# Two wide blocks in place of three narrow ones: re-tiling the expert stage of a fused cross-attention and mixture-of-experts kernel

## The chip, the core and the metric

The kernel runs on one core of a Trainium2 chip. Its engines work side by side, each on its own queue of instructions: TensorE (PE: matrix products and transposes, written to PSUM), VectorE (DVE), ScalarE (ACT), GpSimd (POOL, which here issues gathers and scatters by index) and SyncE (SP, which here issues the plain DMAs). PSUM has 8 banks of 512 fp32 numbers per partition. The metric is the time of one execution on the device in microseconds (us); the kernel before takes 9008.61 us (median of 3 runs, 9005.31 to 9009.49).

## The reference

Everything is fp32. `x` is 4 x 1024 tokens of width 1024. The first layer adds an attention map of each token, computed against a context. The second layer, which takes nearly all the time, is a mixture of 8 experts, of which each token uses 2:

```python
x = x + attention(layernorm(x), ctx_512, ...)
...
router_probs = softmax(x_flat @ gate_w)
topk_w, topk_idx = top_k(router_probs, 2)
topk_w = topk_w / sum(topk_w, axis=-1)
# each token goes to its two experts, sorted by expert
h = silu(ragged_dot(x_rep_sort, w1, group_sizes)) * ragged_dot(x_rep_sort, w3, group_sizes)
out_sort = ragged_dot(h, w2, group_sizes)
out = einsum('tkd,tk->td', out_rep, topk_w)
```

`w1` and `w3` are 1024 x 3584 for each expert, `w2` is 3584 x 1024. The 4096 tokens make 8192 token-expert pairs. On these inputs the router gives the eight experts 984, 991, 1080, 994, 1047, 1004, 1046 and 1046 of them.

## The kernel before

**First part** (up to about 500 us): layer norms, attention, the router, and lists of slots: which token sits where in which expert. At its end small DVE operations on one row (L513 to L564) work out for each expert a *run*: the expert, its first slot and its kind, where a kind is a pair (blocks, width) out of the table `RUNS` (L23). A kind holds blocks x width tokens; the smallest that holds an expert's tokens is taken. Before, the large kinds are three blocks of a width in steps of 8.

**Expert stage** (L566 on). A loop over the runs (L896) switches on the kind (L900) into code unrolled for that kind, `run(i, ex, s0, blocks, width)` (L794). Every matrix product is done by Strassen's scheme in Winograd's form: 7 products of half size, `p1` to `p7`, in place of 8. The tokens of a block are split into two halves of n = width / 2 columns, the other two dimensions into halves as well. So each product has n columns of moving operand, a stationary tile of 128 x 128, and needs sums of weights (`weight_sums`, L627, four DVE operations on a loaded tile) and sums of tokens. fp32 products are two MATMUL instructions each.

A block has two stages:

- *Stage 1* (L813): for each of NI = 14 pairs of 128 hidden units, w1 and then w3: load a weight tile of 1 MB (SP), make its sums, do 7 products of 4 steps of the contraction each (L825), and put the result together from PSUM with `combine` (L657: one ACT copy, four DVE adds). Then silu (ACT), times (DVE), and `token_sums` (L645) stores seven planes of the hidden tile `g`: four quarters, of which one is overwritten by a sum, and three sums.
- *Out-projection* (L853): for each of DQ = 4 quarters of the output width, the 14 pairs in *units* of a weight tile (`W2K`: 8, 8, 6 and 6 times 128 hidden units), 7 products a pair (L864) accumulated over all pairs, `combine`, and for each tile of 128 tokens (`tokens_out`, L767) two transposes on PE (L774), a DVE operation that scales and adds them to `acc` (L776), and, after the last quarter, a scatter to the output by POOL (L780). `acc` was gathered from the output at the end of stage 1 (L851), since another expert may have written there.

The next block's tokens are gathered by POOL into `rows` at the block's begin (L811), or, for the next run's first block, after stage 1 (L844, `load_first`: rows and the first weight tiles `w1a` and `w3a`, which have buffers of their own). `tokens_in` (L737) transposes them on PE into `x` in the out-projection, behind the second quarter. These steps, transposes in and out, stand in a list `late` and are taken from it one by one between products, after each pair of the out-projection or each product group of stage 1. What is left over at the end of a run is done by the next run (`leftover`, L791), after the last run behind the loop.

**What sets the order.** PE's order is as written (`manual_schedule`, L901). On the other engines the framework orders the instructions when it builds the program, and each engine's queue is then executed in order. PSUM: six banks for product groups (a group takes four, two products to a bank except `p1`), two for transposes. Weight tiles go round in three buffers. At the loop's end all engines meet before the next run begins.

Of the kernel before, what the change touches and what calls it, by code (L numbers as in the profile page):

```python
# [19 lines left out]
P = 128  # L20
N = 512

RUNS = [(1, 192), (1, 376), (2, 288), (2, 376), (3, 288)]  # L23
RUNS += [(3, w) for w in range(320, 377, 8)]
# [10 lines left out]
def kernel(  # L35
# [540 lines left out]
    with ExitStack() as st:  # L576
        fst = st.enter_context(tc.tile_pool(name="fst", bufs=1))
        wp = st.enter_context(tc.tile_pool(name="wp", bufs=3))
        hp = st.enter_context(tc.tile_pool(name="hp", bufs=1))
        gp = st.enter_context(tc.tile_pool(name="gp", bufs=2))  # L580
        ip = st.enter_context(tc.tile_pool(name="ip", bufs=2))
        ps = st.enter_context(tc.tile_pool(name="ps", bufs=6, space=PSUM))
        pst = st.enter_context(tc.tile_pool(name="pst", bufs=2, space=PSUM))
# [4 lines left out]
        W2K = [8, 8, 6, 6]  # L588
# [3 lines left out]
        XW = RT * P  # L592
        assert all(w // 2 <= NM and w <= XW for _, w in RUNS)


        T1, B11, B12, B21, B22, T2, T4 = range(7)
        T3 = B12
# [9 lines left out]
        def load(wf, ex, k0, kn, c0):  # L607
            t = wp.tile([P, KD, QW], F32, tag="w", name="wt")
            weights(t, wf, ex, k0, kn, c0)
            return t  # L610

        def factors(t, kn, halves, s):

# [13 lines left out]
        def weight_sums(t, kn, halves, s=None):  # L627
            if s is None:
                s = wp.tile([P, 3, HK, P], F32, tag="s", name="ws")
            f = factors(t, kn, halves, s)  # L630
            a11, a12, a21, a22 = f["p1"], f["p2"], f["p7"], f["p4"]
            nc.vector.tensor_tensor(f["p5"], a21, a22, ALU.add)  # L632
            nc.vector.tensor_tensor(f["p6"], f["p5"], a11, ALU.subtract)  # L633
            nc.vector.tensor_tensor(f["p3"], a12, f["p6"], ALU.subtract)  # L634
            nc.vector.tensor_tensor(a21, a11, a21, ALU.subtract)  # L635
            return f

        RIGHT = dict(p1=B11, p2=B21, p3=B22, p4=T4, p5=T1, p6=T2, p7=T3)
        BANK = dict(p1=(0, 0), p2=(1, 0), p6=(1, 1), p5=(2, 0), p7=(2, 1), p3=(3, 0), p4=(3, 1))
        ENDS = ["p1", "p6", "p7", "p4"]  # L640
# [4 lines left out]
        def token_sums(v, n):  # L645

            def two(a, b):
                return v[..., a : b + 1 : b - a, :]

            nc.vector.tensor_tensor(two(T1, T3), two(B12, B22), two(B11, B12), ALU.subtract)  # L650
            nc.vector.tensor_tensor(v[..., T2, :], v[..., B22, :], v[..., T1, :], ALU.subtract)
            nc.vector.tensor_tensor(v[..., T4, :], v[..., B21, :], v[..., T2, :], ALU.subtract)

        def banks():
            return [ps.tile([P, N], F32, tag="ps", name=f"ps{i}") for i in range(4)]

        def combine(pp, n, c, wide):  # L657

            def pair(t):
                return t[:, : 2 * n].rearrange("p (a b) -> p a b", b=n)  # L660

            def twice(v):
# [3 lines left out]
            nc.scalar.copy(p1s, pp[0][:, :n])  # L666
            nc.vector.tensor_tensor(pair(c), pair(pp[1]), twice(p1s), ALU.add)  # L667
            vu = gp.tile([P, 2, n], F32, tag="vu", name="vu")
            nc.vector.tensor_tensor(vu, pair(pp[2]), twice(c[:, n : 2 * n]), ALU.add)  # L669
            mid = c[:, n : 2 * wide - n].rearrange("p (a b) -> p a b", b=wide - n)[:, :, :n]  # L670
            nc.vector.tensor_tensor(mid, pair(pp[3]), vu, ALU.add)  # L671
            nc.vector.tensor_tensor(  # L672
                c[:, wide + n : wide + 2 * n], pp[2][:, :n], vu[:, 1, :], ALU.add
            )

# [32 lines left out]
        rd0 = fst.tile([P, RT], I32, name="rd0")  # L708
        rows = [fst.tile([P, D], F32, name=f"rows{s}") for s in range(RT)]
        w1a = fst.tile([P, KD, QW], F32, name="w1a")  # L710
        w3a = fst.tile([P, KD, QW], F32, name="w3a")
# [221 lines left out]
```

## Time and profile before

| | us |
|---|---|
| three runs of the kernel | 9008.61 (9005.31 to 9009.49) |
| the profiled execution | 9005.26 |
| its span, first to last instruction | 9003.5 |
| up to the first product of the first run | 535.4 |
| first run (n = 164) / second (168) / third (180) | 999.2 / 1022.7 / 1093.7 |
| between two runs | 10.4 to 11.2 |
| after the last run's products | 16.9 |

The profile is of one execution; all times in it are of that one. Busy time of PE is no measure of its speed, since matmuls overlap: what counts is the distance from one start to the next. Columns of a group are: line, engine, operation, output and inputs with their shapes, count, busy us, mean ns of one, and idle time of the engine before them with what ended it. The mean granted clock of PE over the whole span was 0.987 of full speed.

### The profile page before, as it was taken

How to read it: one execution, taken by the hardware profiler on the slowest of the kernel's cores; microseconds unless marked ns; L12 is line 12 of the kernel's file. 1: busy time of each engine (PE TensorE's matmuls, PEld its weight loads, DVE VectorE, ACT ScalarE, POOL GpSimd, SP SyncE). 2: the span in 40 equal slices, each digit the busy share in tenths (PEclk: the TensorE clock that was granted, in tenths of full speed). 3: DMA queues.
4: the chain of work that ended last, by engine and by line, in shares of the span. 5: the costliest groups of instructions: out<-in, count | busy, mean ns of one | idle time of the engine just before them, and what ended most of it. 6: DMA issues, size and time to landing. Idle time of an engine off the chain costs nothing. (4 is left out here: it accounts for less than half of the span.)

```text
span 9003.5 us, 140017 instructions
## 1 busy us (share of the span) xinstructions
PE 8812.5 (98%) x59462; PEld 8651.3 (96%) x59463; DVE 5109.8 (57%) x10101; ACT 698.5 (8%) x1528; POOL 412.4 (5%) x496
## 2 busy tenths in 40 slices
PE   8979999999999999999999999999999999999999
PEld 5579999999999999999999999999999999999999
DVE  5665655655655655556556556456565565555554
ACT  3310000000000000000000000000000000000000
POOL 2310000000000000000000000000000000000000
PEclk9989999999999999999999999999999999999999
DMA  3234444444443444444444434444444444434343
GB/s 139 109 132 145 139 147 146 138 149 136 154 130 120 144 135 139 133 139 141 142 134 143 142 124 137 145 131 151 142 145 133 129 140 137 140 129 144 125 140 126
DMA packets 1115213, 1236.38 MB, mean 137 GB/s; under 512 B 35312, under 2 KB 1075184, under 8 KB 1114416
## 3 DMA queue, kind: packets, MB, share of 16 engines
q1 hardware_dynamic: 1081616, 1118.37, 38.3%
q0 software_dynamic: 32656, 107.24, 3.4%
q8 instruction: 501, 8.21, 0.4%
q14 instruction: 296, 2.42, 0.1%
q10 hardware_dynamic: 144, 0.13, 0.0%
HBM read 1155.26 MB, written 73.53 MB: 136 GB/s over the span
## 5 line engine op out<-in xcount | busy, mean ns | idle before, releaser
L825 PE MATMUL ps<-x,wt 128*128 128x168 f32 (+3 forms) x15744 | 2510.6, 309 | 0.0
L825 PEld LDWEIGHTS ps<-x,wt 128*128 128x128 f32 x15744 | 2351.7, 190 | 0.0
L864 PE MATMUL ps<-g,wt 128*128 128x168 f32 (+3 forms) x10752 | 2070.9, 309 | 0.0
L632 DVE TENSOR_TENSOR ws<-wt 128x512 f32<-128x512 f32 (+1 forms) x1040 | 693.7, 667 | 2120.1 <-DMA wt<-in_L_ffn_w_dram 2042.2
L864 PEld LDWEIGHTS ps<-g,wt 128*128 128x128 f32 x10752 | 1691.4, 190 | 0.0
L825 PE MATMUL ps<-xs,ws 128*128 128x168 f32 (+3 forms) x10624 | 1659.2, 309 | 0.0
L864 PE MATMUL ps<-g,ws 128*128 128x168 f32 (+3 forms) x8064 | 1615.3, 309 | 0.0
L825 PEld LDWEIGHTS ps<-xs,ws 128*128 128x128 f32 x10624 | 1579.0, 190 | 0.0
L864 PEld LDWEIGHTS ps<-g,ws 128*128 128x128 f32 x8064 | 1294.7, 190 | 0.0
L667 DVE TENSOR_TENSOR c<-ps,p1s 128x352 f32<-128x352 f32 (+3 forms) x672 | 346.5, 516 | 1030.9 <-PE ps L825 1000.1
L825 PE MATMUL ps<-x,ws 128*128 128x168 f32 (+3 forms) x5312 | 883.2, 309 | 0.0
L825 PE MATMUL ps<-xs,wt 128*128 128x168 f32 (+3 forms) x5248 | 872.5, 309 | 0.0
L825 PEld LDWEIGHTS ps<-x,ws 128*128 128x128 f32 x5312 | 804.0, 190 | 0.0
L825 PEld LDWEIGHTS ps<-xs,wt 128*128 128x128 f32 x5248 | 794.3, 190 | 0.0
L633 DVE TENSOR_TENSOR ws<-ws,wt 128x512 f32<-128x512 f32 (+1 forms) x1040 | 692.0, 665 | 28.4
L635 DVE TENSOR_TENSOR wt<-wt 128x512 f32<-128x512 f32 (+1 forms) x1040 | 685.7, 659 | 0.0
L634 DVE TENSOR_TENSOR ws<-wt,ws 128x512 f32<-128x512 f32 (+1 forms) x1040 | 684.6, 658 | 0.0
L666 ACT COPY p1s<-ps 128x168 f32<-128x168 f32 (+3 forms) x768 | 228.2, 297 | 4658.8 <-PE ps L864 2341.3
L836 ACT ACTIVATE c<-c 128x672 f32<-128x672 f32 (+3 forms) x336 | 261.5, 778 | 2648.0 <-DVE c L671 2626.8
L671 DVE TENSOR_TENSOR c<-ps,vu 128x352 f32<-128x352 f32 (+3 forms) x672 | 344.6, 513 | 28.5 <-PE ps L825 20.8
L669 DVE TENSOR_TENSOR vu<-ps,c 128x352 f32<-128x352 f32 (+3 forms) x672 | 342.3, 509 | 5.7 <-PE ps L825 5.6
L699 POOL DMA_INDIRECT rows<-h_d,rd x75 | 79.7, 1063 | 4880.1 <-DVE ws L633 2278.0
(186 smaller groups left out, 3746.1 us busy)
## 6 DMA issues: line engine op xcount, KB each, us to landing
wt<-in_L_ffn_w_dram SPq DMA_DIRECT2D x848, 1024.0 KB, 5.1
wt<-in_L_ffn_w_dram SPq DMA_DIRECT2D x192, 768.0 KB, 4.7
xt<-in_x_dram SPq DMA_DIRECT2D x32, 512.0 KB, 4.3
out_dram<-x SPq DMA_DIRECT2D x32, 512.0 KB, 2.9
h_d<-hn SPq DMA_DIRECT2D x32, 512.0 KB, 2.6
w1a<-in_L_ffn_w_dram SPq DMA_DIRECT2D x9, 1024.0 KB
w3a<-in_L_ffn_w_dram SPq DMA_DIRECT2D x9, 1024.0 KB
cx<-in_ctx_dram SPq DMA_DIRECT2D x4, 1024.0 KB
```

Of the source, the lines that this page charges most:

```text
L632: nc.vector.tensor_tensor(f["p5"], a21, a22, ALU.add)
L633: nc.vector.tensor_tensor(f["p6"], f["p5"], a11, ALU.subtract)
L634: nc.vector.tensor_tensor(f["p3"], a12, f["p6"], ALU.subtract)
L635: nc.vector.tensor_tensor(a21, a11, a21, ALU.subtract)
L666: nc.scalar.copy(p1s, pp[0][:, :n])
L667: nc.vector.tensor_tensor(pair(c), pair(pp[1]), twice(p1s), ALU.add)
L669: nc.vector.tensor_tensor(vu, pair(pp[2]), twice(c[:, n : 2 * n]), ALU.add)
L671: nc.vector.tensor_tensor(mid, pair(pp[3]), vu, ALU.add)
L699: nc.gpsimd.indirect_dma_start(out=dst, out_offset=None, in_=src, in_offset=bass.IndirectOffsetOnAxis(ap=rd[:n, s : s + 1], axis=0),)
L825: nc.tensor.matmul(pp[bk][:, ts(half, n)], left[p][:, k, :], right[p][:, k, :], start=(k == 0), stop=(k == HK - 1),)
L836: nc.scalar.activation(c1, c1, AF.Silu)
L864: nc.tensor.matmul(pp[bk][:, ts(half, n)], left[p][:, k, :], g[:, i2, RIGHT[p], :], start=(i2 == 0 and half == 0), stop=(i2 == NI - 1 and ...
```

## The change

The large kinds are two blocks of a width from 480 to 564 in steps of 4. Each of the seven products has a PSUM bank (seven banks, the eighth for transposes). `rows` takes the part of `acc` too, `w1a` and `w3a` go, and the weights go round in three fixed buffers, into which the first two tiles of the next run are loaded behind the last load of a run. The hidden tile `g` has four planes in place of seven; three sums are made in the out-projection, for each pair and each quarter again (`hidden_factors`), into four small buffers. The units of the out-projection are 4, 6, 6, 6 and 6 times 128; in the last of them the products are done product by product, in the others pair by pair. The next rows are gathered at the fifth pair of stage 1 in both cases, transposed from the start of the out-projection on, and each tile of `rows` is then filled from the output. There are five row tiles, the last of 64 rows, where there were three.

```diff
-RUNS = [(1, 192), (1, 376), (2, 288), (2, 376), (3, 288)]
-RUNS += [(3, w) for w in range(320, 377, 8)]
+RUNS = [(1, 192), (1, 376), (1, 564), (2, 376), (2, 432)]
+RUNS += [(2, w) for w in range(480, 565, 4)]
...
-        wp = st.enter_context(tc.tile_pool(name="wp", bufs=3))
+        tp = st.enter_context(tc.tile_pool(name="tp", bufs=4))
...
-        ps = st.enter_context(tc.tile_pool(name="ps", bufs=6, space=PSUM))
-        pst = st.enter_context(tc.tile_pool(name="pst", bufs=2, space=PSUM))
+        ps1 = st.enter_context(tc.tile_pool(name="ps1", bufs=1, space=PSUM))
+        ps2 = st.enter_context(tc.tile_pool(name="ps2", bufs=3, space=PSUM))
+        pst = st.enter_context(tc.tile_pool(name="pst", bufs=1, space=PSUM))
...
-        W2K = [8, 8, 6, 6]
+        W2K = [4, 6, 6, 6, 6]
+        WR = 3
...
+        ROWS = [P, P, P, P, P // 2]
...
         def banks():
-            return [ps.tile([P, N], F32, tag="ps", name=f"ps{i}") for i in range(4)]
+            one = ps1.tile([P, N], F32, tag="ps1", name="ps1")
+            two = [ps2.tile([P, 2, N], F32, tag="ps2", name=f"ps2_{i}") for i in range(3)]
+            pp = dict(p1=one)
+            for t, (a, b) in zip(two, (("p2", "p6"), ("p5", "p7"), ("p3", "p4"))):
+                pp[a], pp[b] = t[:, 0, :], t[:, 1, :]
...
         rows = [fst.tile([P, D], F32, name=f"rows{s}") for s in range(RT)]
-        w1a = fst.tile([P, KD, QW], F32, name="w1a")
-        w3a = fst.tile([P, KD, QW], F32, name="w3a")
-        s1a = fst.tile([P, 3, HK, P], F32, name="s1a")
+        wts_in = [fst.tile([P, KD, QW], F32, name=f"w{j}") for j in range(WR)]
+        sums_in = [fst.tile([P, 3, HK, P], F32, name=f"s{j}") for j in range(WR)]
...
-        acc = [fst.tile([P, D], F32, name=f"acc{s}") for s in range(RT)]
-        for a in acc:
-            nc.vector.memset(a, 0.0)
...
+        def hidden_factors(v, n):
+
+            t = tp.tile([P, 3, n], F32, tag="t", name="t")
+            t2 = t[:, 0, :]
+            nc.vector.tensor_tensor(t2, v[:, B22, :], v[:, T1, :], ALU.subtract)
+            nc.vector.tensor_tensor(
+                t[:, 1:3, :], v[:, B11 : B21 + 1 : B21 - B11, :],
+                t2.unsqueeze(1).to_broadcast([P, 2, n]), ALU.subtract,
+            )
...
-                if not last:
-                    load_rows(s0 + (b + 1) * width)
-                g = hp.tile([P, NI, 7, n], F32, tag="g", name="g")
+                g = hp.tile([P, NI, 4, n], F32, tag="g", name="g")
...
-                    token_sums(g[:, i2, :, :], n)
+                    nc.vector.tensor_tensor(
+                        v[:, T1, :], v[:, B12, :], v[:, B11, :], ALU.subtract
+                    )
+                    if i2 == RT - 1:
+                        assert not late
+                        load_rows(first_slot(i + 1) if last else s0 + width)
                 if last:
-                    load_first(i + 1)
...
-                for s, r in enumerate(split):
-                    gather(acc[s][:r, :], of, rd, s, r)
+                def rows_of_out(s):
+                    if s < len(split):
+                        gather(rows[s][: split[s], :], of, rd, s, split[s])
+
+                late += tokens_in(rows_of_out)
+                if not last:
+                    late.append(lambda: token_factors(n))
                 for q in range(DQ):
...
+                    for u, kn in enumerate(W2K):
+                        j = load(w2f, 2 * i2, kn, q * QW)
+                        left = weight_sums(j, kn, True)
+                        todo = [
+                            (p, k) for k in range(kn // 2) for p in ORDER
+                        ] if u < len(W2K) - 1 else [
+                            (p, k) for p in ORDER for k in range(kn // 2)
+                        ]
+                        if last and q == DQ - 1 and u == len(W2K) - 1:
+
+                            assert j % WR == WR - 1 == 2
+                            load_first(i + 1, 0)
+                            load_first(i + 1, 1)
+                            late.append(lambda: weight_sums(0, KD, False))
+                        hid = [hidden_factors(g[:, i2 + k, :, :], n) for k in range(kn // 2)]
+                        for at_m, (p, k) in enumerate(todo):
+                            nc.tensor.matmul(
+                                pp[p][:, :n], left[p][:, k, :], hid[k][p],
+                                start=(i2 + k == 0), stop=(i2 + k == NI - 1),
+                            )
+                            if late and at_m % 7 == 6 and i2 + at_m // 7 > 0:
                                 late.pop(0)()
+                        i2 += kn // 2
...
-                    if q == 1:
-                        late += tokens_in()
...
-        load_first(0)
+        load_rows(first_slot(0))
+        load_first(0, 0)
+        load_first(0, 1)
```

In `tokens_in`, each odd step (the DVE copy of a row tile's second half) is followed by `then(s)`, which is `rows_of_out`. `combine` reads the three two-bank tiles with the same operations as before, the single-width add now ahead of the last double one. The last quarter's leftover steps number five.

## The prediction

> **What bounds the kernel now.** I read the page's totals first, then busy time by stretch, then the chain of waits, then single rows.
>
> ```profile
> span 9003.5 us, 140017 instructions
> PE 8812.5 (98%) x59462; PEld 8651.3 (96%) x59463; DVE 5109.8 (57%) x10101; ACT 698.5 (8%) x1528; POOL 412.4 (5%) x496
> ```
>
> TensorE is busy nearly all the time; nobody else comes near. The stretches (columns: us, then busy us and count of PE, PEld, DVE, ACT, POOL, then granted clock, DMA share, GB/s) show a run, the gap behind it, another run, and what follows the last run:
>
> ```profile
> 535.40:1534.60 999.20, 999.20 (x7200) 998.93 (x7200) 585.32 (x1147) 63.38 (x149) 30.26 (x27) 1.00 0.45 145
> 1534.60:1545.80 11.20, 0.31 (x4) 0.07 (x2) 2.04 (x6) 0.00 (x0) 0.00 (x0) 0.67 0.05 12
> 2579.10:3672.80 1093.70, 1093.67 (x7199) 1092.93 (x7200) 608.75 (x1147) 67.64 (x149) 30.35 (x27) 1.00 0.42 134
> 8986.60:9003.50 16.90, 1.60 (x8) 0.70 (x7) 2.48 (x6) 0.00 (x0) 2.98 (x3) 0.59 0.21 83
> ```
>
> So a run has no hole on PE at all, at full clock; holes are the seven gaps of 10.4 to 11.2 us between runs. The time is the prologue to 535.4, eight runs, seven gaps, a tail. Only what PE itself is given to do counts in the runs. How long does it take per instruction? The chain of waits (start, us, what):
>
> ```profile
> 8274.62 8.35 PE ps L825 x56
> 8282.98 0.22 PE pt_y L774 x2
> 8283.20 8.36 PE ps L825 x56
> ```
>
> A product group is 28 products, each two MATMULs: 56 at width 176 in 8.355 us, 149.2 ns each. For wider ones the prologue has fp32 rows (source view with min/median duration, and timeline):
>
> ```profile
> L250 PE MATMUL pm_kv<-wkT,cT x128: 379/379/635, 13.1 to 309.9; 128*128 128x256 f32 x128
> L298 PE MATMUL pm_o<-pT,kv x256: 592/592/1201, 32.7 to 404.3; 128*128 128x512 f32 x128
> ...
> 199.65 1.03 PE L250 MATMUL pm_kv<-wkT,cT 128*128 128x256 f32 x4
> 209.96 1.88 PE L323 MATMUL sim<-kvT,oT 128*128 128x512 f32 x4
> ```
>
> Start to start is (1.03 - 0.379)/3 = 217 ns at 256 columns and (1.88 - 0.592)/3 = 429 ns at 512. From 176 to 512: (429.3 - 149.2)/336 = 0.8335 ns a column, and 149.2 - 176 x 0.8333 = 2.5 ns fixed; at 256 that gives 215.8, as seen. The law is **n/1.2 + 2.5 ns**. Check on whole runs: a run of 3 blocks has 3 x 2352 = 7056 such MATMULs (784 + 392 products a block, twice). At n = 164: 7056 x 139.2 = 982.0 of 999.2; at n = 180: 7056 x 152.5 = 1076.0 of 1093.7. The rest, 17.2 and 17.7 us, is 144 transposes at 0.11 us (0.22 for the pair above) and a slow start.
>
> By Perfetto Trace Analysis (the Trainium skill), section on the most-contended engine, LDWEIGHTS busy time and not matmul busy time tells the distance from the limit. Here that is 96%, so by the rule a third fewer loads would be worth up to a third of 8651 us, and the sum would be near 6100. The rows disagree: spacing follows the columns of the moving operand, 149 to 429 ns for the same load of 128 columns.
>
> **The change, part by part.**
>
> *1. Widths and blocks.* The reference's routing of these inputs gives the experts 984, 991, 1080, 994, 1047, 1004, 1046, 1046 tokens. Before: three blocks of n = w/2 = 164, 168, 180, 168, 176, 168, 176, 176 (the widths of the trace), sum 1376. After: two blocks, w = count/2 rounded up to 4: n = 246, 248, 270, 250, 262, 252, 262, 262, sum 2052. MATMULs take 7056 x (1376/1.2 + 8 x 2.5) = 8232 us before and 4704 x (2052/1.2 + 20) = 8138 after: **-94 us**; 47 of it is padding (2352 x 24/1.2), 47 the fixed 2.5 ns of 18,816 MATMULs fewer. All of it lies on PE, the path that sets the end.
>
> *2. Transposes on PE.* Into x: 24 a block x 24 blocks at 0.11 = 63 us before; after, 16 blocks x (32 + 8 with 64 rows), 63 (a half-size one at half) to 70 us. Out of y: 8 x 36 x 2 before; four runs now have four row tiles and four have five, and 4 x 33 + 4 x 40 = 292 steps replace 288: +1. Together +1 to +8, taken **+3**.
>
> *3. Prologue.* The transposes there go through two PSUM buffers before, through one after (timeline of PE, then of ACT: start, us, what, idle time before):
>
> ```profile
> 524.40 4.27 PE L743 MATMUL pt_h<-ident,rows 128*128 128x128 f32 x20 [25.05 <-DMA rows<-h_d,rd]
> 529.01 0.66 PE L743 MATMUL pt_h<-ident,rows 128*128 128x128 f32 x4 [0.34 <-DVE x L749]
> ...
> 525.57 0.59 ACT L751 COPY x<-pt_h 128x512 f32<-128x512 f32 x1 [30.59 <-DMA w3a<-in_L_ffn_w_dram]
> ```
>
> From 524.40 to the last copy's end at 530.39 (DVE's 0.69 at 529.70) six steps take 6.0 us, overlapped. With one buffer a step is transposes + copy + some 0.15 us of signals: 0.60 (1.06 at the slow clock of the start) + 0.59 or 0.69 + 0.15. Eight full steps and two of half size: 13.0 to 17.5 us, so +7 to +11.5. The two extra gathers hide behind these steps. The run tables get 14 more rows of three small DVE operations, 0.077 us apart at best (the twelve rows there took 4.2 us, shared with other work, 0.35 each): +3.2 to +4.9; three memsets of 0.91 us standing in the same chain go: -2.7, y1's grows by 0.35, and 0.8 us of idle before the first memset takes some up. Together +6 to +14, taken **+10**.
>
> *4. Tail.* POOL scatters the last rows one after the other, each behind the landing of the one before:
>
> ```profile
> 8989.89 1.01 POOL L780 DMA_INDIRECT out_dram<-acc,ids  x1 [138.04 <-DVE acc L776]
> 8994.04 0.99 POOL L780 DMA_INDIRECT out_dram<-acc,ids  x1 [3.14 <-DMA out_dram<-acc,ids]
> 8998.17 0.98 POOL L780 DMA_INDIRECT out_dram<-acc,ids  x1 [3.13 <-DMA out_dram<-acc,ids]
> ```
>
> Five row tiles make five scatters, 4.14 us apart: **+8**. Inside runs the same chain (20 us) lies under stage 1 and ends before the new rows are gathered at pair 4, over 100 us in.
>
> *5. DVE in the out-projection.* The sums of g are no longer stored but made for each quarter q again:
>
> ```profile
> L632 DVE TENSOR_TENSOR ws<-wt 128x384 f32<-128x384 f32 x192 | 107.2, 558 | 583.8 <-DMA wt<-in_L_ffn_w_dram 583.8
> L650 DVE TENSOR_TENSOR g<-g 128x352 f32<-128x352 f32 x126 | 66.1, 525 | 4.1
> L651 DVE TENSOR_TENSOR g<-g 128x176 f32<-128x176 f32 x126 | 43.0, 342 | 4.1
> L776 DVE SCALAR_TENSOR_TENSOR acc<-pt_y,ids,acc 128x256 f32<-128x256 f32 x203 | 97.1, 479 | 1.8 <-PE pt_y L774 1.8
> ```
>
> From 176 to 352 elements 183 ns more: 1.04 ns an element. At n = 262 a pair's two operations take 0.43 + 0.70 = 1.13 us. A quarter: PE 196 MATMULs x 220.8 = 43.3 us; DVE 14 x 1.13 = 15.8 hidden sums, weight sums 4 x 2.2 + 1.7, combine 2.5, five reads of transposes 2.4: 31.2 us, 72%. Hidden by PE's matmuls, and four buffers keep the sums a unit (9.3 us) ahead. Cost 0; without cover it would be what exceeds 43.3.
>
> *6. PSUM.* All eight banks are bound, none spare. At a quarter's end the last add to be done (0.70 us after the last product) frees the bank that the next quarter writes with its sixth product, 5 x 0.44 = 2.2 us on: 1.3 us of slack. Each transpose step inside the runs must find its one bank read out by the next, 14 x 220.8 = 3.09 us later. Over all reads of pt_y before, the median from the last transpose's start to the read's end is 1.1 us, nineteen in twenty are below 2.6, the longest is 3.8. With 376 such steps in the out-projections, 0 (all under 3.09) to 376 x 0.1 = 38 us; taken **+5**, since the rows lie nearly all under the limit.
>
> Perfetto Trace Analysis, section Matmuls (the Trainium skill), speaks against this part: matmul groups should rotate through banks so that one is emptied while the next fills. By it every step with a lone bank waits for its copy; by the rows of this trace, nothing, as the next use is 3 us off. No run here shows a lone bank yet.
>
> *7. Order of loads.* The next run's two first weights go on SP's queue behind the run's last load, into slots 0 and 1 of the ring. Slot 1 comes free when the last unit starts, 9.3 us before the run's end, and a 1 MB load lands 5.1 us after its issue by the page: 4 us of cover. Nothing of the run stands behind it on SP. The first sums of the next run (four DVE operations of 0.69) sit in that last unit. Rows for the next block move from the out-projection to pair 4 of stage 1, and the rows of the output are gathered by POOL behind each tile's transposes, read some 10 us or more later. Cost 0; bounds -2 to +20 over the gaps (up to 2.5 us each if landing doubles).
>
> **Sum**: -94 + 3 + 10 + 8 + 0 + 5 + 0 = -68. The profiled execution took 9005.26 us (its span 9003.5), 3.4 below the median 9008.6. So about 8937 for it and **8941** for a median. Own range of this case: all low ends -94 + 1 + 6 + 8 + 0 - 2 = -81 (8927); high ends -94 + 8 + 14 + 8 + 38 + 20 = -6, though hardly all at once; 8927 to 8962.
>
> **Rivals.** About 0.2% (18 us) is what a measurement of this kernel can tell from no change.
> - *DVE becomes the bound of the out-projection* (slower). The place is every quarter. Other work there is 15.4 us, so it decides when the hidden sums cost over (43.3 - 15.4)/15.8 = 1.77 times my price. With broadcast and strided operands at twice the price: 15.4 + 31.6 - 43.3 = 3.7 us x 64 quarters = 237, so 9178. Against: L667 broadcasts p1s and takes 524 ns at 352 elements, as L650. Chance 0.06.
> - *The lone transpose bank holds PE up*: 376 steps at 0.15 us more, 56, so near 8995. For: DVE reads at 72% load, in order, and waits on DMA before weight sums (L632's idle time). Against: the latencies above. At 0.1 it is 8974. Chance 0.13, mostly at the lower end.
> - *The gaps grow*, the first weights landing after the end: 8 x 3 = 24 us, 8965. Against: 4 us of cover. Chance 0.07.
> - *The fixed 2.5 ns doesn't go*, the change being only padding: 8941 + 47 = 8988. Against: the rows at 256 and 512. Chance 0.04.
>
> **Numbers.** Forecast 0.70. The range 8925 to 8983 takes in the two middle rivals. Faster by over 0.2% (below 8991): 0.70 + 0.10 + 0.07 + 0.02 = 0.89. Within 0.2%: 0.05. Slower: 0.06.
>
> **What would show it.** MATMULs of form 128x246 to 128x270 spaced 207.5 to 227.5 ns; runs of 4704 of them with some 17 us beside; no hole on PE in a run; DVE's hidden sums near 430 and 700 ns; a transposing stretch of 13 to 17 us before the loop; five scatters at the end; gaps between runs of 10 to 11 us. Wrong would make it: holes on PE at the units' starts waiting for DVE (the first rival), before transposes (the second), or gaps over 12 us (the third).

## The result, and the profile after

The changed kernel takes 8945.33 us (median of four runs, 8943.72 to 8949.42), the kernel before 9006.96 (four runs, 9004.79 to 9009.49). The ratio is 0.9932, with a 95% interval of 0.9916 to 0.9948: faster by 0.7%. The forecast was 8941.

The page's totals of the changed kernel:

```profile
span 8941.9 us, 99381 instructions
PE 8736.7 (98%) x40738; PEld 7530.9 (84%) x40739; DVE 4822.9 (54%) x8820; ACT 666.7 (7%) x1170; POOL 446.1 (5%) x512
```

A third of the instructions on PE is gone, and the busy time of weight loads fell by 1120 us, from 96% to 84% of the span. The span fell by 61.6 us. PE itself is at 98% as before: nearly the same number of columns goes through it.

Busy time by stretch of the changed kernel (us, then busy us and count of PE, PEld, DVE, ACT, POOL, granted clock, DMA share, GB/s): a run, the gap behind it, another run, what follows the last run, and the last out-projection.

```profile
545.90:1541.50 995.60, 995.20 (x4850) 905.82 (x4850) 549.54 (x979) 59.54 (x104) 32.88 (x27) 1.00 0.31 99
1541.50:1552.00 10.50, 0.33 (x3) 0.04 (x1) 0.93 (x2) 0.00 (x0) 0.00 (x0) 0.77 0.04 9
2567.00:3657.30 1090.30, 1090.30 (x4864) 906.41 (x4864) 574.59 (x986) 63.39 (x104) 34.75 (x30) 1.00 0.29 94
8917.30:8941.90 24.60, 3.54 (x12) 1.25 (x10) 3.11 (x6) 0.00 (x0) 4.89 (x5) 0.55 0.21 87
8736.40:8917.30 180.90, 180.90 (x854) 154.49 (x853) 111.29 (x218) 4.23 (x9) 6.15 (x5) 1.00 0.31 98
```

The two runs shown are 3 to 4 us shorter than their counterparts before, at full clock and still full; their columns add up to the same as before (2 x 246 = 3 x 164, 2 x 270 = 3 x 180). So do those of the sixth run (2 x 252 = 3 x 168), which is 5 us shorter; the other five, with fewer columns, are 12 to 18 us shorter. The gap is 10.5 us where it was 11.2; the tail is 24.6 us where it was 16.9. Cut at the starts of the first and last products of each run, the two profiled executions (spans 9003.5 and 8941.9) come apart like this:

| piece | before, us | after, us | difference | predicted |
|---|---|---|---|---|
| up to the first product of the first run | 535.4 | 545.9 | +10.6 | +10 |
| the eight runs | 8376.5 | 8296.2 | -80.3 | -86 |
| the seven gaps between them | 74.7 | 75.2 | +0.5 | 0 |
| after the last product | 16.9 | 24.6 | +7.7 | +8 |
| span | 9003.5 | 8941.9 | -61.6 | -68 |

The chain of waits of the changed kernel (start, us, what), in its last out-projection:

```profile
8835.10 0.22 PE pt_y L783 x2
8835.32 3.09 PE ps L894 x14
8838.42 0.22 PE pt_y L783 x2
```

Fourteen MATMULs between two transposes at width 262 take 3.09 us, 220.8 ns each, which is 262/1.2 + 2.5. This is the period at which the one transpose bank is used.

The chain of waits says only PE here. The view of what waited for whom, from 560 to 8900 us, says what little else there is (engine, tile and line, what ended the wait: sum us, count, longest us):

```profile
PE ps L838 <- issue: 72.5, 7, 10.8
...
PEld pt_h L737 <- issue: 9.4, 28, 0.4
PEld ps L838 <- DVE c L665: 2.7, 4, 0.8
PEld pt_h L737 <- DVE x L757: 1.3, 4, 0.3
...
PEld ps L894 <- DVE y L672: 0.4, 1, 0.4
```

Seven gaps, and then little: no wait for a transpose bank that would reach the list (in the runs, no `pt_y` line), and five short ones for a product bank. The 28 + 4 stops of PEld at `pt_h` are the 32 places at which a row tile of 64 rows is transposed; they matter below, in step 2.

### The profile page after: what moved, and what is told of

Its sections match the earlier page's. It is cut to its first block, busy times and chain, and to the rows that moved or that the text cites. A ratio compares the mean times of both kernels' runs of the same rounds, so it can differ in the third digit from the quotient of the medians.

```text
span 8941.9 us, 99381 instructions
## 1 busy us (share of the span) xinstructions
PE 8736.7 (98%) x40738; PEld 7530.9 (84%) x40739; DVE 4822.9 (54%) x8820; ACT 666.7 (7%) x1170; POOL 446.1 (5%) x512
## 5 line engine op out<-in xcount | busy, mean ns | idle before, releaser
L838 PE MATMUL ps<-x,w 128*128 128x262 f32 (+5 forms) x10752 | 2489.2, 381 | 78.9 <-issue 77.8
L838 PEld LDWEIGHTS ps<-x,w 128*128 128x128 f32 x10752 | 2043.9, 191 | 370.3 <-issue 80.6
L838 PE MATMUL ps<-xs,s 128*128 128x262 f32 (+5 forms) x7168 | 1625.9, 379 | 0.0
L838 PEld LDWEIGHTS ps<-xs,s 128*128 128x128 f32 x7168 | 1355.0, 189 | 195.1
L894 PE MATMUL ps<-g,s 128*128 128x262 f32 (+5 forms) x3584 | 1026.1, 379 | 0.0
L894 PE MATMUL ps<-t,w 128*128 128x262 f32 (+5 forms) x3584 | 1024.9, 379 | 0.0
L894 PE MATMUL ps<-g,w 128*128 128x262 f32 (+5 forms) x3584 | 904.6, 381 | 0.0
L838 PE MATMUL ps<-xs,w 128*128 128x262 f32 (+5 forms) x3584 | 848.2, 379 | 0.0
L838 PE MATMUL ps<-x,s 128*128 128x262 f32 (+5 forms) x3584 | 848.2, 380 | 0.0
L672 DVE TENSOR_TENSOR c<-ps,vu 128x524 f32<-128x524 f32 (+5 forms) x448 | 309.8, 691 | 919.7 <-PE ps L838 919.7
L894 PEld LDWEIGHTS ps<-g,s 128*128 128x128 f32 x3584 | 680.1, 190 | 95.3 <-DVE y L672 0.4
L838 PEld LDWEIGHTS ps<-x,s 128*128 128x128 f32 x3584 | 680.9, 190 | 94.1
L838 PEld LDWEIGHTS ps<-xs,w 128*128 128x128 f32 x3584 | 678.6, 189 | 96.4
L894 PEld LDWEIGHTS ps<-t,w 128*128 128x128 f32 x3584 | 678.8, 189 | 96.1
L766 DVE TENSOR_TENSOR t<-g 128x262 f32<-128x262 f32 (+5 forms) x896 | 375.5, 424 | 677.1 <-PE ps L894 674.0
L894 PEld LDWEIGHTS ps<-g,w 128*128 128x128 f32 x3584 | 651.4, 190 | 76.6
L894 PE MATMUL ps<-t,s 128*128 128x262 f32 (+5 forms) x1792 | 512.9, 380 | 0.0
```

The costliest lines, as they stand in the source:

```text
L672: nc.vector.tensor_tensor(mid, qc[:, :, :n], vu, ALU.add)
L766: nc.vector.tensor_tensor(t2, v[:, B22, :], v[:, T1, :], ALU.subtract)
L838: nc.tensor.matmul(pp[p][:, :n], left[p][:, k, :], right[p][:, k, :], start=(k == 0), stop=(k == HK - 1),)
L894: nc.tensor.matmul(pp[p][:, :n], left[p][:, k, :], hid[k][p], start=(i2 + k == 0), stop=(i2 + k == NI - 1),)
```

## The experiments

Twelve kernels ran, among them the changed kernel itself again (`e0_after`). They ran in four groups, each on one chip beside the kernel before, whose medians were 9008.22, 9006.29, 9008.03 and 9005.07 us in the four. Times are medians; ratios, where given, are to the kernel before with their 95% interval.

**The changed kernel again**, as the yardstick of its group.

> The changed kernel itself, as the base beside the others of this call. Theory and rivals alike: 8945, span 8942 to 8946.

Measured: 8947.56 us (8943.31 to 8950.62), ratio 0.9934 (0.9917 to 0.9950), span 8941.5. It repeats the result.

**Only the padding undone.** Widths in steps of 12 give each run as many columns as before (over the eight runs 2 x 2064 = 4128, as the 3 x 1376 before, against 2 x 2052 = 4104 with steps of 4), with blocks as wide as in the change.

```diff
-RUNS += [(2, w) for w in range(480, 565, 4)]
+RUNS += [(2, w) for w in range(480, 565, 12)]
```

> Widths in steps of 12 in place of 4. The eight runs then have n = 246, 252, 270, 252, 264, 252, 264, 264, sum 2064, and 2 x 2064 = 4128 is just the number of columns that the three-block kernel had (3 x 1376). Theory (PE's time is columns/1.2 + 2.5 ns an instruction, nothing else moves): 4704 x 12/1.2 = 47 us more than the changed kernel, less 0 to 3 us for 14 table rows fewer: 8989 to 8992, and still 15 to 18 below the kernel before, which is the fixed cost of 18,816 instructions (47) less prologue, tail and transposes. Rival (the gain is slack of DVE or of the loads, not columns): 8945, as the changed kernel.

Measured: 8988.51 us (8984.05 to 8991.82), ratio 0.9978 (0.9969 to 0.9988), span 8990.1. The eight runs sum to 8343.0 us against 8295.5 of `e0_after`: 47.5 us more, where 24 columns fewer in 2352 MATMULs at 1/1.2 ns are 47.0. So the padding is one half of the products' 94 us. The other half is what is left without it: these runs are 33.5 us shorter than the 8376.5 us before, although transposes cost them some 12 us and bank waits 2 us more (step 2 and step 6 below), which makes some 47 us for the products. Without the padding the whole change would have brought 0.2%.

**Three narrow blocks in the new structure.** The table of runs of the kernel before, with everything else of the change kept: seven banks, hidden sums in each quarter, trailing loads.

```diff
-RUNS = [(1, 192), (1, 376), (1, 564), (2, 376), (2, 432)]
-RUNS += [(2, w) for w in range(480, 565, 4)]
+RUNS = [(1, 192), (1, 376), (2, 288), (2, 376), (3, 288)]
+RUNS += [(3, w) for w in range(320, 377, 8)]
...
-        ROWS = [P, P, P, P, P // 2]
+        ROWS = [P, P, P]
```

> The changed kernel with the old table of kinds, three blocks of 328 to 360 tokens, three row tiles. Theory (PE sets the time, the rest of the structure is neutral): products +94, six steps in the prologue in place of ten -6, table rows -3 to 0, tail -8, transposes in the runs -9: 8945 + 94 - 24 = about 9013 (9005 to 9018). Rival (the structure needs the wide blocks, since DVE makes the hidden sums in each quarter whatever the width: 14 x 0.87 + 10.6 + 1.9 + 1.4 = 26.0 us of DVE in a quarter of 29.2 us of PE, 89%, in order behind loads): holes on PE at the units of the out-projection; at 0.5 us a quarter and 96 quarters 9060.

Measured: 9085.37 us (9082.45 to 9090.48), ratio 1.0086 (1.0069 to 1.0103). In this kernel the third block of a run takes the second block's tokens again, so its work is of the right amount and its tokens are not. The theory (9005 to 9018: the structure costs nothing and saves nothing) missed by 70 us. The rival, by which the structure needs the wide blocks, had 9060 and was nearer. Of its reason one half, DVE busy for 89% of a quarter, doesn't hold: 89.5 of 122.9 us and 92.7 of 122.4 us in two out-projections are 73 and 76%. The other half, that DVE works in order behind loads, is what the traces below show. The next kernel gives the third block its own tokens:

```diff
-                        load_rows(first_slot(i + 1) if last else s0 + width)
+                        load_rows(first_slot(i + 1) if last else s0 + (b + 1) * width)
```

> The three-block kernel again, now with the third block's own tokens (the run before took the second block's tokens for the third, in the same number of instructions). If the time doesn't hang on the data: 9085 (9082 to 9090), with holes on PE of 6 to 10 us a run and gaps of 12.6 to 13.2 us between runs. If it does: the 9005 to 9018 of the first theory.

Measured, with this line on top of the edit above: 9079.36 us (9075.76 to 9085.44), ratio 1.0077 (1.0060 to 1.0094), just under the 9082 to 9090 expected, so the wrong tokens were not the reason. Against the profiled kernel before, the span is 80 us longer: the seven gaps sum to 88.6 us instead of 74.7 (+14), the runs to 8438.0 instead of 8376.5 (+61), the prologue is 4 longer, the tail 1. Beside those of the gaps, its main waits, between 560 and 8900 us:

```profile
PE ps L838 <- DVE c L669: 23.2, 21, 2.4
PEld ps L894 <- DVE y L672: 19.3, 44, 0.5
```

There are two places. L894 waits for L672 at the quarters' starts, for the bank that the last drain of the quarter before frees (a drain is the operation that empties a bank). At 176 columns the next quarter's sixth product, which needs it, comes 5 x 2 x 0.149 = 1.5 us after its first, at 262 columns 2.2 us. The timeline of one such place (start, us, what, idle time before):

```profile
5779.83 0.56 DVE L633 TENSOR_TENSOR s<-w 128x384 f32<-128x384 f32 x1 [1.80 <-DMA w<-in_L_ffn_w_dram]
...
5780.81 0.76 PE L894 MATMUL ps<-g,w 128*128 128x176 f32 x4
...
5782.18 0.52 DVE L672 TENSOR_TENSOR y<-ps,vu 128x352 f32<-128x352 f32 x1
...
5782.75 0.57 PE L894 MATMUL ps<-g,s 128*128 128x176 f32 x2 [0.23 <-DVE y L672]
```

The quarter's first product starts at 5780.81, and L672 ends 1.9 us behind it. In DVE's queue it stands behind weight sums whose load had come late. L838 waits for L669 in stage 1, and one such place shows the same:

```profile
3017.94 0.69 DVE L633 TENSOR_TENSOR s<-w 128x512 f32<-128x512 f32 x1 [5.55 <-DMA w<-in_L_ffn_w_dram]
...
3019.87 0.53 DVE L667 TENSOR_TENSOR vu<-ps,c 128x360 f32<-128x360 f32 x1
3020.31 0.68 DVE L635 TENSOR_TENSOR s<-w,s 128x512 f32<-128x512 f32 x1
3020.91 0.34 DVE L669 TENSOR_TENSOR c<-ps,vu 128x180 f32<-128x180 f32 x1
...
3021.40 1.46 PE L838 MATMUL ps<-xs,s 128*128 128x180 f32 x8 [1.18 <-DVE c L669]
```

DVE stood for 5.55 us at a weight sum whose weights had not landed. The operations that empty the banks (L667, L669) are behind it in the same queue, and the other sums of that load, 0.7 us each, run ahead of them or between them. PE, out of banks, waited 1.18 us. DVE had been idle before: it is the order on it, and the landing, that held PE up. The changed kernel has the same order and the same wait for a load, with a wider cover; one of the four holes of its stage 1:

```profile
1662.25 0.69 DVE L633 TENSOR_TENSOR s<-w 128x512 f32<-128x512 f32 x1 [8.97 <-DMA w<-in_L_ffn_w_dram]
1662.86 0.67 DVE L665 TENSOR_TENSOR c<-ps,p1s 128x496 f32<-128x496 f32 x1
1663.58 1.94 PE L838 MATMUL ps<-x,w 128*128 128x248 f32 x8 [0.46 <-DVE c L665]
```

That these loads come late because their buffers come free late was not tried.

**The longer gaps of three blocks.** In `e10_three_blocks` the last packet of the second trailing load ends 0.3 to 0.9 us before the run's last product starts; in the changed kernel 3.2 to 4.2 us before. A longer last unit issues it earlier:

```diff
-        W2K = [4, 6, 6, 6, 6]
+        W2K = [4, 4, 6, 6, 8]
```

> The three-block kernel (own tokens) with units of 4, 4, 6, 6 and 8 times 128 in place of 4, 6, 6, 6 and 6: the last unit lasts 8.0 us in place of 6.0 at width 168, so the next run's second tile lands some 2.7 us before the run's end instead of 0.7. Theory (a gap of 12.6 us instead of 10.6 comes of that load's landing close to the end): gaps back to 10.4 to 11.2 us. Rival (the gap is longer for another reason, such as three blocks' code): 12.2 to 13.1 as before. The holes at the quarters should grow in either case, as the last unit now holds all four buffers of hidden sums.

Measured, on top of `e10_three_blocks`: 9047.08 us (one run; the kernel before 9005.07 beside it). The last packets now end 2.4 to 3.1 us ahead, and the gaps are 10.5 to 10.9 us again (sum 75.0 instead of 88.6). So the gap of 12.2 to 13.1 us goes with the late load, as the theory had it, and not with three blocks. Why it costs 2 us is open. By the signals of its landing, the late load is complete 0.0 to 0.9 us *behind* the start of the last product, the earlier one 1.6 to 2.4 us ahead of it; but the seven gaps don't grow with the delay, and no run separates the landing from what SP has still to do behind its issue.

The expectation that the holes at the quarters would grow was wrong: holes in the out-projections fell from 31.9 to 9.8 us, while those in stage 1 stayed (29.1 and 31.7). This settles where the holes at the quarters came from. The widths are the same, and so is the time to the sixth product. But in `e10_three_blocks` a weight sum that had waited for its load stands ahead of L672 at all 72 starts of a quarter that follows another, and L672 ends 1.3 to 2.1 us after the quarter's first product; with the new units it does so at none of the 72, and L672 ends 0.8 us after it (start, us, what; the first product here, then L672):

```profile
5756.44 0.76 PE L894 MATMUL ps<-g,w 128*128 128x176 f32 x4
...
5756.74 0.52 DVE L672 TENSOR_TENSOR y<-ps,vu 128x352 f32<-128x352 f32 x1
```

In the changed kernel, at 1 of 48 such starts a weight sum stands ahead, and that is the one place of the list with a wait for L672. The 9.8 us left in the out-projections are another thing: PE waits there ten times for a hidden sum (L766).

**The hidden sums, more often.** The first of a pair's two operations twice (`e3_small_twice`), then both twice (`e4_both_twice`, the edit shown), then both three times (`e9_thrice`):

```diff
+            for _ in range(2):
+                nc.vector.tensor_tensor(t2, v[:, B22, :], v[:, T1, :], ALU.subtract)
+                nc.vector.tensor_tensor(
+                    t[:, 1:3, :], v[:, B11 : B21 + 1 : B21 - B11, :],
...
```

> The first of the two hidden sums (128 x n, 0.42 us) is made twice, with the same result. Theory (DVE has 12 us of slack in a quarter of 43.3 us): DVE goes to (31.2 + 14 x 0.42) = 37.1 of 43.3 us, 86%, and the time stays: 8945 to 8950. Rival (the in-order queue of DVE is already near its limit, so that added work shows): 0.42 us x 896 = up to 376 more, 9000 to 9320.

Measured: 8946.47 us (two runs), ratio 0.9934 (0.9914 to 0.9954), DVE busy 5152 us instead of 4823. No change of time, as the theory had it.

> Both hidden sums are made twice, with the same result. Theory: 15.4 + 31.6 = 47.0 us of DVE in a quarter of 43.3 us of PE; the 3.7 us over stand on PE's path, 64 quarters: 8945 + 237 = 9182 (9130 to 9240). Rival (DVE's slack is larger than counted, since operations overlap by some 0.09 us each): 5 to 7% less DVE time, 44 us, so 8945 to 9000.

Measured: 8945.61 us (two runs), ratio 0.9933 (0.9913 to 0.9953). My theory (9182) fell altogether: 820 us more work on DVE (busy 5642.8 us instead of 4822.9) cost nothing. The last out-projection of this kernel, as in the stretches above:

```profile
8738.50:8919.40 180.90, 180.90 (x855) 154.66 (x853) 160.16 (x322) 4.23 (x9) 5.79 (x5) 1.00 0.31 98
```

DVE is busy 160.16 of 180.90 us there instead of 111.29 (166.55 instead of 118.62 in another block), and PE has no hole. A block's 52 more pairs add 48.9 us, 0.94 each, though the operations of a pair last as predicted. By form (line, engine, operation, tiles, count, then busy us and mean ns), of the changed kernel at width 262:

```profile
L767 DVE TENSOR_TENSOR t<-g,t 128x524 f32<-128x524 f32 x336 | 233.7, 700 | 6.0
L766 DVE TENSOR_TENSOR t<-g 128x262 f32<-128x262 f32 x336 | 142.8, 430 | 279.8 <-PE ps L894 278.8
```

430 + 700 is 1.13 us, not 0.94. The timeline of DVE in `e4_both_twice` (start, us, what) shows where the difference goes:

```profile
8853.56 0.41 DVE L767 TENSOR_TENSOR t<-g 128x262 f32<-128x262 f32 x1
8853.90 0.54 DVE L634 TENSOR_TENSOR s<-s,w 128x384 f32<-128x384 f32 x1
8854.37 0.69 DVE L768 TENSOR_TENSOR t<-g,t 128x524 f32<-128x524 f32 x1
8854.99 0.41 DVE L767 TENSOR_TENSOR t<-g 128x262 f32<-128x262 f32 x1
```

Each starts 0.07 us before the end of the one ahead of it, of which it needs nothing: 0.34 us after the start of one of 0.41, 0.47 after one of 0.54, 0.62 after one of 0.69. Durations in a row sum to more than the time they take.

> Both hidden sums are made three times, with the same result. Made twice, DVE was busy for 160 to 167 of the 181 us of an out-projection, 49 more than once. Theory (PE sets the time until DVE's own work exceeds it): 209 to 216 of 181 us, 28 to 35 over, 16 blocks: 8945 + 500 = 9445 (9390 to 9510). Rival (DVE may catch up in stage 1, where it is busy for half the time): less than half of it, below 9200.

Measured: 9498.12 us (one run), the runs 554 us longer than in the changed kernel. Its waits, between 560 and 9400 us:

```profile
PE ps L895 <- DVE t L767: 350.2, 190, 4.2
```

Now PE waits for the hidden sums. An estimate from the two measured occupancies puts the bound at 1 + (180.9 - 111.3)/48.9 = 2.4 times their price, or 2.3 times from a block with 118.6 us of other and own work; no kernel between two and three times ran.

**The trailing loads undone.** The next run's first weights are loaded at that run's own start.

```diff
-                        j = load(wf, 0, KD, i2 * QW, there=ahead)
-                        left = (factors if loads == 1 else weight_sums)(j, KD, False)
+                        j = load(wf, 0, KD, i2 * QW)
+                        left = weight_sums(j, KD, False)
...
-                            load_first(i + 1, 0)
-                            load_first(i + 1, 1)
-                            late.append(lambda: weight_sums(0, KD, False))
```

> The next run's two first weight tiles are not loaded behind the last load of a run, but at the run's own begin, like any other tile; the sums of the first tile too. Theory (the loads behind the last unit hide a landing of 5.1 us and sums of 2.8 us): each run's first product waits for the landing, 5 to 6 us after PE is there, and its third product for the sums behind them, 0 to 3 us; 8 runs x 5 to 9 = 40 to 72: 8985 to 9017. Rival (the code loading and the meeting of the engines between runs hide a load anyway): 8945 to 8955.

Measured: 8985.62 us (8982.63 to 8990.85), ratio 0.9976 (0.9966 to 0.9986); gaps of 16.6 to 17.9 us (sum 119.0 against 74.6), the runs as they were (8295.2 against 8295.5). From the timeline of its first gap:

```profile
1552.41 3.35 SPq L606 DMA_DIRECT2D w<-in_L_ffn_w_dram  x3
...
1559.38 1.17 PE L838 MATMUL ps<-x,w 128*128 128x248 f32 x2 [17.56 <-DMA w<-in_L_ffn_w_dram]
```

SP issues its first load of the run 10.6 us after the last product ends, and the first product follows 7 us on. In the changed kernel PE starts at 1551.99 in this place. So the trailing loads are worth 6.3 us a gap; they do not shorten a gap of the kernel before, which had its own early loads. Of the 10 to 11 us that stay in the changed kernel, the profile puts none to a load; it names no releaser for them.

**The prologue's transposes in three banks.** Before the first run the product banks are idle; the transposes go through them.

```diff
-                pt = pst.tile([P, 4, P], F32, tag="pt", name="pt_h")
+                if spare:
+                    pt = ps2.tile([P, 2, N], F32, tag="ps2", name="pt_h")[:, 0, :]
+                    pt = pt.rearrange("p (a b) -> p a b", b=P)
...
-        for step in tokens_in():
+        for step in tokens_in(spare=True):
```

> The ten transposing steps ahead of the loop write in turn to the three pairs of product banks, idle there, instead of the one bank for transposes. Theory (the 17 us of that stretch are the turn of one bank: transposes, copy, signals): it falls to ten steps x 0.45 to 0.9 us of PE plus one copy, 6 to 10 us, so 7 to 11 less: 8934 to 8938. Rival (the stretch waits for the gathered rows, 2.25 MB): no change, 8945.

Measured: 8935.23 us (8934.48 to 8937.01), ratio 0.9922 (0.9905 to 0.9939). PE's timeline, first of the changed kernel, then of this one:

```profile
524.09 1.09 PE L737 MATMUL pt_h<-ident,rows 128*128 128x128 f32 x4 [26.09 <-DMA w<-in_L_ffn_w_dram]
...
527.80 1.12 PE L737 MATMUL pt_h<-ident,rows 128*128 128x128 f32 x4 [0.78 <-DVE x L742]
```

```profile
524.95 3.47 PE L741 MATMUL pt_h<-ident,rows 128*128 128x128 f32 x16 [25.63 <-DMA rows<-h_d,rd]
529.28 1.07 PE L741 MATMUL pt_h<-ident,rows 128*128 128x128 f32 x8 [0.86 <-DVE x L746]
531.11 1.76 PE L741 MATMUL pt_h<-ident,rows 128*128 128x128 f32 x16 [0.76 <-DVE x L746]
539.10 2.39 PE L842 MATMUL ps<-x,w 128*128 128x246 f32 x5 [6.22 <-issue]
```

With one bank every four transposes wait some 0.7 us for the copy of the four before and take 1.1 us, to the last full four. With three banks they come in rows of 16, 8 and 16, and the first product comes 14.2 us after the first transpose instead of 21.9.

**The last scatters without their order.** The five scatters at the end write different rows; here they are declared independent of one another.

```diff
-                    nc.gpsimd.indirect_dma_start(
+                    to = nc.gpsimd.indirect_dma_start(
...
+                    if apart:
+                        if outs:
+                            tc.declare_no_dep(to.ins, group="outs", reason="rows are disjoint")
+                        tc.add_to_no_dep_group("outs", to.ins)
+                        outs.append(to)
```

> The five scatters behind the loop no longer wait for each other's landing; an expert's tokens are distinct, so their rows of the output are too. Theory (4.1 us apart, 3.1 of them waiting): four gaps of 3.1 us go, or less where PE and DVE set the pace (1.26 us a step): 8945 - 12 = 8932 to 8935. Rival (the landing itself is the limit, the DMA rings being shared): 8940 to 8945.

Measured: 8935.24 us (8932.74 to 8937.67), ratio 0.9920 (0.9904 to 0.9937). POOL's timeline at the end, first of the changed kernel, then of this one:

```profile
8924.83 0.99 POOL L790 DMA_INDIRECT out_dram<-rows,ids  x1 [3.14 <-DVE rows L785]
8928.93 0.97 POOL L790 DMA_INDIRECT out_dram<-rows,ids  x1 [3.12 <-DMA out_dram<-rows,ids]
```

```profile
8926.55 0.99 POOL L792 DMA_INDIRECT out_dram<-rows,ids  x1 [0.31 <-issue]
8927.85 0.98 POOL L792 DMA_INDIRECT out_dram<-rows,ids  x1 [0.30 <-issue]
```

4.1 us apart become 1.3 us apart; the piece after the last product is 14.1 us instead of 24.6, shorter than in the kernel before with its three scatters (16.9).

**Both together.**

> The product banks for the prologue's transposes and the scatters apart, in one kernel. Theory (two separate stretches, one ahead of the loop and one behind it, on no common resource): the gains of the two runs add, 8.7 and 10.5 us of span: 8946 - 19 = 8927 (8924 to 8930). Rival (each gain is a shift of waiting, which the other takes up): 8935, as one alone.

Measured: 8925.88 us (four runs, 8924.18 to 8930.05), ratio 0.9909 (0.9892 to 0.9925). The two gains, some 10 us each against the changed kernel's 8945.33, add up to 19.5; one lies ahead of the first run (8.4 us from the first transpose to the first product) and the other behind the last (14.1 us instead of 24.6). This is the fastest version: 19 us under the changed kernel.

## Why the prediction was right, step by step

The forecast was 68 us off the time; the spans differ by 61.6. The term of the sum that was mis-sized is step 2, the transposes: 12.7 us where +3 was taken and +8 was the upper bound. The runs' -80.3 is then, to half a us, -94 of products, +12.7 of transposes, +2.4 of waits for banks and about -1 at the runs' starts. That the whole came within 7 us is in part luck: the 9.7 us too little for transposes stand against 2.6 too much for banks and the starts' 1. Nor was the upper end of 8962 worked out: the high ends of the terms add up to -6, which is 9003.

1. *Products, -94.* Right. With n/1.2 + 2.5 ns the 4704 MATMULs of every run come out, and `e1_step12` shows the padding's half by itself: 47.5 us for 47.0. The other half rests on the law's fit to the runs, and on what is left of the gain in `e1_step12`. Perfetto Trace Analysis (the Trainium skill), section Identifying the Most-Contended Engine, has LDWEIGHTS busy share, beside a measure of the useful work, tell how near the limit TensorE is. What a load less is worth it does not say; the third of 8651 us was the prediction's own inference, and it is not borne out: the weight loads' busy time fell by 13%, from 8651.3 to 7530.9 us, and the time by 0.7%. Nor does the share by itself tell the distance here: it fell from 96% to 84%, and PE has next to no hole in the runs of either kernel.
2. *Transposes, +3 taken, +1 to +8 as bounds: measured +12.7.* I let the transposes of the 64-row tile cost something between half and all of a full one. They cost more than a full one, by what lies around them. The timeline of PE in the changed kernel (start, us, what), at one four of full size and one of half size:

```profile
1377.45 0.60 PE L737 MATMUL pt_h<-ident,rows 128*128 128x128 f32 x4
1377.88 1.00 PE L894 MATMUL ps<-g,w 128*128 128x246 f32 x4
1378.72 0.58 PE L894 MATMUL ps<-t,s 128*128 128x246 f32 x2
...
1403.79 0.58 PE L894 MATMUL ps<-t,w 128*128 128x246 f32 x2
1404.30 0.46 PE L737 MATMUL pt_h<-ident,rows 64*128 64x64 f32 x4
1404.69 1.10 PE L894 MATMUL ps<-g,w 128*128 128x246 f32 x4
1405.62 0.58 PE L894 MATMUL ps<-t,s 128*128 128x246 f32 x2
```

   Four full ones take 0.43 us from their start to the next product's (0.437 in the records), and the four products behind them 0.84, as four products should (4 x 0.2075 = 0.83). The half-size four starts 0.51 us after a pair that should take 0.415, takes 0.39, and the four products behind it take 0.93. So it costs 0.094 before, 0.389 itself and 0.104 behind, 0.587 in all against 0.437, at each of the 32 places in the runs. The 128 full fours cost 55.9 us, as 0.437 each; with the 32 half ones that makes 74.7 us where 62.9 were, +11.8. Another +0.9 is out of `y`.

   The weight loads show where the time before goes (the same two places):

```profile
1377.24 0.57 PEld L737 LDWEIGHTS pt_h<-ident,rows 128*128 128x128 f32 x4
...
1404.29 0.32 PEld L737 LDWEIGHTS pt_h<-ident,rows 64*128 64x128 f32 x4 [0.32 <-issue]
```

   A full four's first load starts 0.21 us ahead of its transpose, under the product before. A half four's starts with it, after 0.32 us in which PEld stands: these are the 32 stops of the list. The 0.104 behind is not peculiar to 64 rows: each of the five bank waits in the runs is followed by one interval 0.104 us too long as well.
3. *Prologue, +10: measured +10.6*, by way of two errors that cancel in the two executions compared. The step of one buffer runs at the slow end throughout (1.8 to 1.9 us a step, where I had it quicken as the clock rose), so the stretch from the first transpose to the last copy takes 17.1 us of the 13.0 to 17.5 allowed; to the first product it is 21.9 us instead of 11.0. The tables' extra rows and the memsets together come to nothing in this pair of executions (first transpose at 524.09 us, before 524.40), where I had up to two and a half us. That is not resolved: in eight other executions with the same tables the first transpose starts at 522.7 to 527.1 us, and the close hit of +10.6 is luck to that extent. `e6_front_banks` takes the lone buffer away and gets 8 us back.
4. *Tail, +8: measured +7.7*; two scatters at 4.1 us are 8.2. `e7_scatters_apart` shows that it was the order among them.
5. *DVE, 0.* Right in the time, wrong in the reckoning. I had 72% occupancy in a quarter from a sum of durations; by the stretches it is 62 to 65% over an out-projection, since the operations overlap. For the same reason the rival's turning point, 1.77 times my price, was too low: doubled, the sums still cost nothing; at three times they cost 554 us; the point is at 2.3 to 2.4, by the estimate above.
6. *Banks, +5: measured +2.4*, and not where I looked. The lone transpose bank cost nothing inside the runs: its next use is 3.09 us off and no wait for it shows. Where uses follow one another at once, in the prologue, the rule of Perfetto Trace Analysis (the Trainium skill), section Matmuls, that independent groups should rotate through banks, is borne out: three banks there were worth 8 us. At the quarters' starts there is hardly a hole either: the drain mostly ends 1.1 us after a quarter's first product, and the sixth comes 2.1 to 2.2 us after it (the 1.3 us of slack should have been 1.5 by its own terms, 2.2 less 0.70). What there is lies nearly all in stage 1: four waits of 0.2 to 0.6 us there and one of 0.2 at a quarter, each with the 0.1 behind it, where a drain stood behind a weight sum. In `e0_after` they come to less than 1 us, so 2.4 is this execution's.
7. *Order of loads, 0: measured +0.5 over seven gaps.* The cover of some 4 us that I worked out is the 3.2 to 4.2 us by which the loads land ahead of the end. `e5_late_first` prices the trailing loads at 6.3 us a gap, and `e10_three_blocks` shows the cover nearly used up.

The rivals: DVE becomes the bound only at some 2.3 times the price; the lone transpose bank doesn't hold PE up; the gaps didn't grow; the fixed 2.5 ns went.

What the prediction didn't see is that steps 5 to 7 are not free by themselves. At the old widths the new structure makes the kernel 71 us slower than before (`e10_three_blocks`), in bank waits and gaps; the wide blocks, in the same structure, are then worth some 134 us in the medians, or 102 against `e11_last_unit_8` (one run), whose units suit the narrow blocks better. The 2.4 us of step 6 are what is left of these costs at 246 to 270 columns. What is shown: the longer gaps and the holes at the quarters both go when the units are cut otherwise, at the same widths; those holes come where late weight sums stand ahead of the drain, and a short time to the sixth product alone doesn't make them. The holes of stage 1 stay at narrow blocks and are nearly gone at wide ones; that their loads come late because buffers come free late is not shown. Nor was the 64-row tile transposed at full size in any run: its cost is read from the trace.

## What to carry to other kernels

Where one engine is full, count what it is given to do from start-to-start distances, not its busy time nor the number of its instructions: here a third fewer MATMULs and 1120 us less of weight loads were worth half of 94 us, and padding the other half. Wider tiles do more than save fixed costs: they lengthen the stretches under which drains, loads and recomputed operands lie, and a structure that is nearly free at 250 columns cost 0.8% at 170, some of which another cut of the units won back. Look at the ends too: a few us of transposes through one bank and of scatters in a needless order were worth 19 us, more than all the waits inside the runs.

## What was not expected of the hardware

- DVE operations that don't depend on one another start some 0.07 us before the recorded end of the one ahead. In rows of 0.4 to 0.7 us that is 10 to 17%, so the sum of durations overstates occupancy: a pair of 1.13 us adds 0.94 us.
- Four transposes of 64 rows cost more on a busy PE than four of 128. Among themselves they step at 0.111, 0.064 and 0.062 us where the full ones step at 0.109, but 0.094 us are lost before the first, whose weight load doesn't run ahead, and 0.104 behind the last, 0.587 us in all against 0.437.
- Transposes in fours with a wait for a copy between them took 1.1 us a four through 15 us of the prologue; sixteen in a row there took 3.47 us, and four inside a run 0.437 to the next product. The granted clock was 0.50 over those 17 us (524 to 541), and 0.81 over 8 us with the rows of 16, 8 and 16 (525 to 533). It rose to 0.98 (528 to 531) behind the row of 16, and to 0.99 in the same place behind a row of 20 in the kernel before; with a wait behind every four it stayed where it was, and so the waits cost twice.
- Where the last packet of a run's last load ends 0.3 to 0.9 us before the last product, the gap behind the run is 2 us longer; at 2.4 us and more before it, it isn't. The cause is open.
